# Placing by scatter instead of by matmul, and a new order at the two ends of pass 2

## The chip, the core and the metric

The kernel runs on one core of one Trainium2 chip. The metric is device time in microseconds (us) of one execution. TensorE (PE) multiplies matrices, VectorE (DVE) and ScalarE (ACT) work on rows, GpSimd (POOL) does simple row work and issues indirect DMAs, SyncE (SP) issues plain DMAs. All DMAs share 16 DMA engines.

## The reference, cut to what matters

Four graph layers run one after the other on the same dense float32 adjacency matrix `adj` (2708 x 2708) and features `x` (2708 x 128), each with a residual and a layer norm:

```python
# layer 0: normalised product, 4 nearest neighbours by S, then a second normalised product
z = leaky_relu(lap_mul(A, x) @ W1 + b1, 0.1)
S = exp(-sqrt(max(|zi|^2 + |zj|^2 - 2 zi.zj, 0) + 1e-10) / 2)   # the 4 largest of each row are kept
out0 = lap_mul(S_top4 + A, x) @ W2 + b2          # lap_mul(A, x) = d * (A @ (d * x)), d = 1/sqrt(row sums)
# layer 1: attention over the graph
XW = x @ W; Z = leaky_relu(s_row[:, None] + s_col[None, :], 0.01); den = exp(Z)
num = A @ den
out1 = A @ ((den / num) @ XW)
# layers 2 and 3
out2 = (d * (A @ (d * x))) @ W.T + b;  out3 = relu([x, A @ x] @ W.T + b)
```

In layer 1 `den[i, j]` depends on `s_row[i] + s_col[j]` alone and changes its form where that sum changes sign. If the nodes are sorted by their `s_col` value (`cc` in the kernel), the columns of `den` fall into 43 blocks of 64. For each block most rows keep one form over the whole block; only the few rows whose sign changes inside the block need their own treatment.

## The kernel before, in words

**Passes.** A multiplication with the adjacency matrix is a pass (`by_panels`): `adjT` is walked in C = 6 column chunks (four of 512 columns, one of 384, one of 276). In each chunk T = 22 row tiles of 128 rows (the last of 20) are summed into one PSUM tile `acc`. Rows 0 to 15 come from memory as panels of four tiles (`load_panel`, 1 MB for 512 columns, three buffers, SyncE's queue); rows 16 to 21 stay in SBUF (`res`). So a chunk is 16 matmuls from panels and 6 from `res`, and a 512-column matmul in float32 takes 0.43 us twice.

The stages are: pass 1 with the degrees (L401 to L476), the neighbour search (L524 to L551), pass 2 (L711 to L713), the ranking and pass 3 (L715 to L896), the blocks of the attention (L938 to L968), and three more passes.

**From the search to pass 2.** The search finds for each tile its 4 nearest neighbours (`near`, `where`) by MAX8 and FIND_INDEX8 on VectorE. `weigh(ts)` computes the weights and `y2 = d2inv * x` for a group of tiles and writes these rows to DRAM (`y2_rows`), three times: tiles 0 to 16, 17 to 19, and 20 to 21. The writes are issued from ScalarE's queue (L514, L518). In pass 2, GpSimd gathers four neighbours' rows for every tile from `y2_rows` by indirect DMA (`sum_near`, L571, 88 of them, 16 buffers), and VectorE adds them up (`near_sum`). The first three panels of pass 2 are loaded ahead (`ready`, L520).

**The order by hand.** In pass 2 TensorE, VectorE and ScalarE keep program order (`manual_schedule`). The order is written with `Due`: each pass matmul is a tick, and work is due at a tick. `near_at` says when `sum_near` of a tile is due, and `end_pass2` lays out what follows a finished chunk: `finish` (adds `near_sum` and copies to `hT`), `norm0` (second weight and layer norm), `turn` (transposes), `find_c` (the value `cc` on all partitions, in `c_row`), and for each tile `compare` (which `cc` are at least as large: a mask on VectorE, L664), `times_w` (L651), `rank_rows` (ScalarE adds up the mask's rows, L675) and `rank_columns` (TensorE adds up its columns into `rk`, L680). For the last tile VectorE adds up the rows itself while it makes the mask (L659).

**Ranks, block lists and pass 3.** `rk_f` (L735) is every node's place in the order of `cc`. From it VectorE finds each node's block (`blk`), the weights of pass 3 (`lc`, two columns for each block, in the buffer tagged `wide` that `xwe` had before) and the node's place in the list of its block (`pos`). The lists (`slot_i`, `slot_e`, `slot_f`) are made by matmuls: VectorE writes a 0/1 matrix `at` for each tile (L813) and TensorE multiplies it with the values `val_b` (L814). The order itself is made likewise (`at` L846, matmul L847 with `val_q`), which gives `jidx` (the node at each rank) and `csort` (its `cc`). `xwe` (the rows of XW) is written to `xw_rows`, and 22 indirect DMAs gather its rows in order into `xws` (L857). `rows_from` (L228) puts `csort` and `rr` on all partitions by 44 transposes, for `g_row` and `gb`; `lw` (L865) is made from `g_row`.

Outside pass 2 a scheduler decides the program order of each engine. Pass 3 (L896) multiplies with `lc` and gives `carry`; it runs beside the work of the last paragraph. Then, for each block, GpSimd gathers the list's rows of the matrix (L950), TensorE multiplies them with `lw` (L963), and `mix` divides and multiplies with `xws` (L889).

Of the kernel before, what the change touches and what calls it, by code (L numbers as in the profile page):

```python
# [8 lines left out]
F32 = mybir.dt.float32  # L9
U32 = mybir.dt.uint32  # L10
# [40 lines left out]
def kernel(  # L51
# [105 lines left out]
    def by_panels(weights, done, tick=None, ready=()):  # L157

        ready = list(ready)
        for c in range(C):
            w = cw[c]
            acc = acc_tile()
            for i in range(T):
                if i < S:
                    if i % 4 == 0:
                        part = ready.pop(0) if ready else load_panel(i // 4, c)
                    src = part[:, i % 4, :w]
                else:  # L170
                    src = res[: pw[i], i - S, cols[c]]
                lhsT = weights(i)
                nc.tensor.matmul(  # L173
                    acc[: lhsT.shape[-1], :w], lhsT=lhsT, rhs=src, start=(i == 0), stop=(i == T - 1 and tick is None)
                )
                if i == T - 1:
                    done(c, acc)
                if tick is not None:
                    tick()
# [40 lines left out]
    def rows_from(dst, col, ts, exp_scale=None):  # L220

        ts = list(ts)
        for g in range(0, len(ts), 4):
            grp = ts[g : g + 4]
            ps = mis_tile()
            w = 0
            for t in grp:
                nc.tensor.transpose(  # L228
                    ps[:, w : w + pw[t]], col[: pw[t], t : t + 1].to_broadcast([pw[t], P]), ident[: pw[t], : pw[t]]
                )  # L230
                w += pw[t]
            if exp_scale is None:
                evacuate(g // 4, dst[:, g * P : g * P + w], ps[:, :w])
            else:
                nc.scalar.activation(dst[:, g * P : g * P + w], ps[:, :w], AF.Exp, scale=exp_scale)

# [17 lines left out]
    jidx = att1.tile([P, NQ], U32, tag="jidx", name="jidx")  # L254
# [56 lines left out]
    with tc.tile_pool(name="knn", bufs=1) as knn:  # L311
# [180 lines left out]
        def weigh(ts):  # L492
# [21 lines left out]
            nc.scalar.dma_start(  # L514
                y2_rows[t0 * P : full * P, :].rearrange("(t p) d -> p t d", p=P), y2[:, t0:full, :]
            )
            if full < t1:
                nc.scalar.dma_start(y2_rows[FULL * P :, :], y2[:LAST, FULL, :])  # L518
# [3 lines left out]
        with tc.tile_pool(name="keys", bufs=3) as keys:  # L522
# [28 lines left out]
            weigh(range(T - 2, T))  # L551
# [8 lines left out]
    xwe = wide.tile([P, T, D + 1], F32, tag="wide", name="xwe")  # L560
# [37 lines left out]
    xw_rows = dram.tile([N, D], F32, tag="xw_rows", name="xw_rows")  # L598
# [49 lines left out]
    def times_w(c, t):  # L648
        p, o = pw[t], t * P - starts[c]
        po = mis_tile()  # L650
        nc.tensor.matmul(po[:p, : D + 1], lhsT=xTs[c][:, o : o + p], rhs=wae[:, : D + 1], start=True, stop=True)  # L651
        nc.scalar.copy(xwe[:p, t, :], po[:p, : D + 1])

    def compare(t):
# [3 lines left out]
        if t == T - 1:  # L658
            nc.vector.tensor_scalar(  # L659
                mask[:p, : o + p], c_row[:p, : o + p], s, 0.0, op0=ALU.is_ge, op1=ALU.add,  # L660
                accum_out=rows_m[:p, t : t + 1],
            )
        else:
            nc.vector.tensor_scalar(mask[:p, : o + p], c_row[:p, : o + p], s, None, op0=ALU.is_ge)  # L664
# [5 lines left out]

    def rank_rows(t):
        p, w = pw[t], t * P + pw[t]
        if t < T - 1:
            junk = sum_pool.tile([P, N], BF16, tag="copy", name="junk")
            nc.scalar.activation(junk[:p, :w], masks[t][:p, :w], AF.Copy, accum_out=rows_m[:p, t : t + 1])  # L675
# [12 lines left out]
    near_at = [31 + 4 * t for t in range(4)] + [44 + (24 * (t - 4)) // 5 for t in range(4, 15)]  # L688
    near_at += [100, 106, 113, 120, 128, 135, 142]
# [3 lines left out]
    def end_pass2(c, acc):  # L693
        n = max(T * (c + 1), near_at[chunk_tiles[c][-1]] + 3)

# [5 lines left out]
        at(n + 2, norm0, chunk_tiles[c])  # L701
        at(n + 9, turn, c)
        at(n + 11, find_c, c)
        for k, t in enumerate(chunk_tiles[c]):
            at(n + 13 + 2 * k, compare, t)
            at(n + 14 + 2 * k, times_w, c, t)
            at(n + 16 + 2 * k, rank_rows, t)
            if t:
                at(n + 19 + 2 * k, rank_columns, t)

    with tc.manual_schedule(engines={nc.tensor.engine, nc.vector.engine, nc.scalar.engine}):  # L711
        by_panels(rows_of(y2), end_pass2, due.tick, ready)
        due.flush()  # L713
    late.close()
    lwx = ctx.enter_context(tc.tile_pool(name="lwx", bufs=1))  # L715
    xws = lwx.tile([P, NQ, D], F32, tag="xws", name="xws")
    lw = lwx.tile([P, NB, BJ], F32, tag="lw", name="lw")
    g_row = hT

    with tc.tile_pool(name="rank", bufs=1) as rank, tc.tile_pool(name="rank2", bufs=2) as rank2:  # L720
# [3 lines left out]
        nc.scalar.dma_start(xw_rows[: FULL * P, :].rearrange("(t p) d -> p t d", p=P), xwe[:, :FULL, :D])  # L724
        if LAST:
            nc.scalar.dma_start(xw_rows[FULL * P :, :], xwe[:LAST, FULL, :D])
        nc.vector.tensor_copy(rr, xwe[:, :, D])
        nc.scalar.activation(e_r, rr, AF.Exp)
        nc.scalar.activation(f_r, rr, AF.Exp, scale=0.01)

# [6 lines left out]
        nc.vector.tensor_add(rk_f[:lp, T - 1 :], after[:lp, T - 1 :], rows_m[:lp, T - 1 :])  # L737

# [18 lines left out]
        lc = wide.tile([P, T, NB, 2], F32, tag="wide", name="lc")  # L757
# [32 lines left out]
        totals = rtile([T, NB], "totals")  # L790
# [16 lines left out]
        val_b = big.tile([P, T, 3, NB], F32, tag="y", name="val_b")  # L807
        for n, v in enumerate((node_oob, e_r, f_r)):
            nc.vector.tensor_mul(val_b[:, :, n, :], in_b, v[:, :, None].to_broadcast(grid))
        sl = mis_tile()  # L810
        for t in range(T):
            at = rank2.tile([P, P], F32, tag="at", name="at")
            nc.vector.tensor_scalar(at, iota, pos[:, t : t + 1], None, op0=ALU.is_equal)  # L813
            nc.tensor.matmul(  # L814
                sl[:, : 3 * NB], lhsT=at, rhs=val_b[:, t, :, :].rearrange("p a b -> p (a b)"),
                start=(t == 0), stop=(t == T - 1),
            )
        for h in range(2):
            nc.vector.tensor_scalar(
                slot_i[h], sl[:, :NB], 2.0, 2.0 * OOB + h, op0=ALU.mult, op1=ALU.add  # L820
            )

        nc.vector.tensor_scalar_add(slot_e, sl[:, NB : 2 * NB], ident[:, KC : KC + 1])
        nc.vector.tensor_scalar_add(slot_f, sl[:, 2 * NB : 3 * NB], ident[:, KC + 1 : KC + 2])


        rk_i = rtile([T], "rk_i", I32)
        nc.vector.tensor_copy(rk_i, rk_f)
        hi_i = rtile([T], "hi_i", I32)
        nc.vector.tensor_single_scalar(hi_i, rk_i, 7, op=ALU.arith_shift_right)  # L830
        hi = rtile([T], "hi")
        nc.vector.tensor_copy(hi, hi_i)
        lo = rtile([T], "lo")
        nc.vector.scalar_tensor_tensor(lo, hi, -float(P), rk_f, op0=ALU.mult, op1=ALU.add)
        of_q = rtile([T, NQ], "of_q")
        nc.vector.tensor_tensor(
            of_q, hi[:, :, None].to_broadcast([P, T, NQ]), iota[:, None, :NQ].to_broadcast([P, T, NQ]),
            op=ALU.is_equal,
        )
        val_q = big.tile([P, T, 2, NQ], F32, tag="y", name="val_q")  # L840
        nc.vector.tensor_mul(val_q[:, :, 0, :], of_q, node[:, :, None].to_broadcast([P, T, NQ]))
        nc.vector.tensor_mul(val_q[:, :, 1, :], of_q, cc[:, :, None].to_broadcast([P, T, NQ]))
        js = mis_tile()
        for t in range(T):
            at = rank2.tile([P, P], F32, tag="at", name="at")
            nc.vector.tensor_scalar(at, iota, lo[:, t : t + 1], None, op0=ALU.is_equal)  # L846
            nc.tensor.matmul(  # L847
                js[:, : 2 * NQ], lhsT=at, rhs=val_q[:, t, :, :].rearrange("p a q -> p (a q)"),
                start=(t == 0), stop=(t == T - 1),
            )  # L850
        nc.vector.tensor_copy(jidx, js[:, :NQ])
        nc.vector.tensor_copy(csort, js[:, NQ : 2 * NQ])
        nc.scalar.activation(g_col, csort, AF.Exp, scale=0.99)
        nc.scalar.activation(g_inv, csort, AF.Exp, scale=-0.99)
        for q in range(NQ):
            p = pw[q]
            nc.gpsimd.indirect_dma_start(  # L857
                out=xws[:p, q, :], out_offset=None, in_=xw_rows[:, :],
                in_offset=bass.IndirectOffsetOnAxis(ap=jidx[:p, q : q + 1], axis=0),
                bounds_check=N - 1, oob_is_err=False,  # L860
            )
            nc.scalar.mul(xws[:p, q, :], xws[:p, q, :], g_col[:p, q : q + 1])
        rows_from(g_row, csort, range(T), 0.99)
        for b in range(NB):
# [3 lines left out]
            )  # L868

    gb = hT  # L870
    rows_from(gb, rr, range(T), 0.99)
    carry = big.tile([P, N], F32, tag="y", name="carry")

    def mix(w, q, num, col, haccs, pool):
# [12 lines left out]
        for o in range(0, w, CW):  # L887
            e = min(w, o + CW)
            nc.tensor.matmul(  # L889
                haccs[:, o:e], lhsT=xws[:p, q, :], rhs=err[:p, o:e], start=(q == 0), stop=(q == NQ - 1)  # L890
# [5 lines left out]
    by_panels(lambda i: lc[: pw[i], i, :, :].rearrange("p b s -> p (b s)"), end_carry)  # L896
    psum.close()
# [74 lines left out]

    mixed = big.tile([P, T, D], F32, tag="y", name="mixed")
# [99 lines left out]
```

## Time and profile before

| | us |
|---|---|
| time, median of 3 runs | 1165.31 (1161.83 to 1165.72) |
| the profiled execution | 1204.79 |
| its span, first to last instruction | 1203.1 |
| TensorE busy in the span | 1088.8 (91%) |
| VectorE busy | 657.8 (55%) |
| ScalarE, GpSimd busy | 317.5, 264.9 |
| pass 2 and its tail, in the span | 291 to 487 |
| pass 3 | 490 to 634 |

All other times in the text come from the profiled execution: they are us from the span's start. A timeline line has the start, the length, engine, source line, operation, the names written and read, the shape, how many instructions are merged, and in brackets how long the engine was idle before it and what ended that. "PE" is a matmul, "PEld" its weight load; an engine's name with a q is its sequencer, which issues DMAs. One matmul of the source is two records in float32. "Granted clock" is TensorE's clock as a share of full speed.

### The profile page before, as it was taken

The numbers are of one execution on the slowest core, as the hardware profiler recorded it, in microseconds if no ns is written. First come the engines' busy times: TensorE is split into PE (matmuls) and PEld (weight loads), VectorE is DVE, ScalarE is ACT, GpSimd is POOL, SyncE is SP. The second block draws the span as 40 slices with busy tenths as digits, with TensorE's granted clock in tenths as the row PEclk, the third lists the DMA queues.
The fourth block names the chain that finished last, engine by engine and source line by source line (L and its number), as shares of the span: only waits on it lengthen the run. The fifth ranks groups of instructions, "written<-read, shape, count | busy, mean of one in ns | idle before, by whom it ended". The sixth has DMA issues, their size and how long they took to land. (4 is left out here: it accounts for less than half of the span.)

```text
span 1203.1 us, 11015 instructions
## 1 busy us (share of the span) xinstructions
PE 1088.8 (91%) x3625; PEld 515.5 (43%) x3625; DVE 657.8 (55%) x1428; ACT 317.5 (26%) x591; POOL 264.9 (22%) x261
## 2 busy tenths in 40 slices
PE   1899999999946995796799999999899999999997
PEld 1355444443423473253243333333344554465445
DVE  6875469999215476843005999999712112123122
ACT  0001145554001245104005566666311010002000
POOL 4000000001574670007014555565001000000000
PEclk9899999999977896798799999999899999999999
DMA  9994410002715461541653453455375675664754
GB/s 351 372 296 170 141 35 0 1 1 89 269 48 173 150 205 41 176 147 46 202 159 117 149 168 113 128 163 166 109 245 180 191 263 184 209 205 142 250 169 121
DMA packets 113714, 190.88 MB, mean 159 GB/s; under 512 B 13334, under 2 KB 51520, under 8 KB 113652
## 3 DMA queue, kind: packets, MB, share of 16 engines
q1 hardware_dynamic: 90872, 151.05, 38.1%
q0 software_dynamic: 17280, 36.31, 9.6%
q10 hardware_dynamic: 5500, 2.77, 0.8%
q8 instruction: 30, 0.49, 0.2%
q14 instruction: 32, 0.26, 0.1%
HBM read 214.34 MB, written 4.16 MB: 182 GB/s over the span
## 5 line engine op out<-in xcount | busy, mean ns | idle before, releaser
L173 PE MATMUL acc<-part,y 128*128 128x512 f32 (+2 forms) x384 | 160.0, 560 | 0.5 <-issue 0.5
L950 POOL DMA_INDIRECT rows<-in_adjT,slot_i x86 | 122.2, 1421 | 148.6 <-PE num L963 69.5
L963 PE MATMUL num<-rows,lw 128*64 128x512 f32 (+2 forms) x516 | 115.7, 557 | 2.8 <-DMA rows<-in_adjT,slot_i 2.8
L889 PE MATMUL hacc<-err,xws 128*128 128x512 f32 (+3 forms) x264 | 112.4, 562 | 2.2 <-DVE err L884 2.2
L543 PE MATMUL acc<-zT,z 128*128 128x512 f32 (+4 forms) x264 | 107.1, 551 | 0.0
L571 POOL DMA_INDIRECT got<-y_rows,where x88 | 93.3, 1060 | 58.3 <-DVE near_sum L577 21.7
L173 PEld LDWEIGHTS acc<-part,y 128*128 128x128 f32 x384 | 71.2, 196 | 69.0 <-issue 61.9
L173 PE MATMUL acc<-part,lc 128*86 128x512 f32 (+2 forms) x192 | 84.6, 585 | 16.4 <-DMA part<-in_adjT 13.9
L882 DVE TENSOR_TENSOR err<-inv,num 128x1024 f32<-128x1024 f32 (+1 forms) x88 | 74.3, 855 | 22.4 <-ACT inv L879 21.0
L878 ACT ACTIVATE inv<-num 128x1024 f32<-128x1024 f32 (+1 forms) x88 | 64.4, 735 | 83.1 <-PE num L963 79.2
L544 ACT COPY key<-acc 128x512 f32<-128x512 f32 (+3 forms) x132 | 70.2, 534 | 58.2 <-issue 29.8
L374 PE MATMUL acc<-part,y 128*128 128x512 f32 (+2 forms) x192 | 82.3, 581 | 2.2 <-DVE y L197 2.2
L889 PEld LDWEIGHTS hacc<-err,xws 128*128 128x128 f32 (+1 forms) x264 | 46.6, 189 | 79.7 <-issue 40.4
L173 PE MATMUL acc<-part,xs 128*128 128x512 f32 (+2 forms) x192 | 77.9, 546 | 0.1
L884 DVE SCALAR_TENSOR_TENSOR err<-hT,g_inv,err 128x1024 f32<-128x1024 f32 (+1 forms) x88 | 77.1, 917 | 0.0
L173 PE MATMUL acc<-part,mixed 128*128 128x512 f32 (+2 forms) x192 | 75.5, 545 | 0.1
L883 DVE SCALAR_TENSOR_TENSOR err<-err,inv 128x1024 f32<-128x1024 f32 (+1 forms) x88 | 71.8, 857 | 0.0
L184 ACT COPY hT<-acc 128x512 f32<-128x512 f32 (+2 forms) x18 | 9.6, 535 | 230.1 <-PE acc L173 230.1
L543 PEld LDWEIGHTS acc<-zT,z 128*128 128x128 f32 (+1 forms) x264 | 46.8, 186 | 54.0 <-issue 48.7
L545 DVE MAX8 near<-key 128x8 f32<-128x2708 f32 (+1 forms) x22 | 65.4, 2972 | 5.1 <-ACT key L544 5.1
L879 ACT ACTIVATE inv<-inv 128x1024 f32<-128x1024 f32 (+1 forms) x88 | 67.3, 768 | 2.6
L508 POOL TENSOR_TENSOR y<-xs,d2inv 128x2176 f32<-128x2176 f32 (+1 forms) x2 | 4.7, 2325 | 277.4 <-ACT d2inv L506 277.4
(230 smaller groups left out, 1270.9 us busy)
## 6 DMA issues: line engine op xcount, KB each, us to landing
part<-in_adjT SPq DMA_DIRECT2D x102, 1024.0 KB
part<-in_adjT SPq DMA_DIRECT2D x24, 768.0 KB
part<-in_adjT SPq DMA_DIRECT2D x24, 552.0 KB
res<-in_adjT SPq DMA_DIRECT2D x4, 1280.0 KB
got<-y_rows,where POOLq DMA_INDIRECT x88
rows<-in_adjT,slot_i POOLq DMA_INDIRECT x86
rows<-carry SPq DMA_DIRECT2D x86, 10.6 KB
xw_rows<-xwe ACTq DMA_DIRECT2D x1, 1344.0 KB
```

The source lines that it names most:

```text
L173: nc.tensor.matmul(acc[: lhsT.shape[-1], :w], lhsT=lhsT, rhs=src, start=(i == 0), stop=(i == T - 1 and tick is None))
L374: nc.tensor.matmul(accs[c][:, : cw[c]], lhsT=y[: pw[i], i, :], rhs=src[: pw[i], : cw[c]], start=first, stop=last)
L543: nc.tensor.matmul(pks[c][:p, : cw[c]], lhsT=z2[:, :p], rhs=zT[:, cs], start=False, stop=True)
L544: nc.scalar.copy(key[:p, cs], pks[c][:p, : cw[c]])
L571: nc.gpsimd.indirect_dma_start(out=got[:p, :], out_offset=None, in_=y2_rows[:, :], in_offset=bass.IndirectOffsetOnAxis(ap=where[:p, t, k : ...
L879: nc.scalar.activation(inv[:p], inv[:p], AF.Exp, scale=-1.0)
L882: nc.vector.tensor_mul(err[:p], inv[:p], num[:p, :w])
L883: nc.vector.scalar_tensor_tensor(err[:p], err[:p], 2.0, inv[:p], op0=ALU.subtract, op1=ALU.mult)
L884: nc.vector.scalar_tensor_tensor(err[:p], gb[:p, col : col + w], g_inv[:p, q : q + 1], err[:p], op0=ALU.max, op1=ALU.mult)
L889: nc.tensor.matmul(haccs[:, o:e], lhsT=xws[:p, q, :], rhs=err[:p, o:e], start=(q == 0), stop=(q == NQ - 1))
L950: nc.gpsimd.indirect_dma_start(out=rows[:KC, n, :], out_offset=None, in_=adj_half[:, :], in_offset=bass.IndirectOffsetOnAxis(ap=slot_i[h][ ...
L963: nc.tensor.matmul(num[n * BJ : n * BJ + bw[b], o:e], lhsT=lw[:, b, : bw[b]], rhs=rows[:, n, c0 + o : c0 + e], start=True, stop=True,)
```

## The change

Four parts:

- **Order and lists by scatters.** The matmuls L814 and L847, their matrices, `jidx`, `xw_rows` and the gathers L857 go. `xwe` gets one more column, for `cc`; 22 indirect DMAs on GpSimd write its rows to `by_rank` in DRAM, each row to the place of its rank, and one load brings them back as `xws`, with `csort` in the last column. Another 22 write three values of each node (12 bytes) to `by_slot`, at the place in its block's list, and one load brings the lists back. `rows_from` gives way to `as_row` (one transpose of 22 rows, exponential, write to DRAM) and `on_all` (one load that repeats the row on all partitions). The 22 scalings of `xws` on ScalarE become one product on GpSimd.
- **`lc` in a buffer of its own**, where it shared the one of `xwe`.
- **Last rows ahead.** `weigh` writes tiles 20 and 21 from SyncE's queue, and the first panel load of pass 2 that isn't loaded ahead stands behind that write (`behind`). The other two writes move to GpSimd's queue. In chunk 0 of pass 2 four resident tiles (16 to 19) come before tiles 12 to 15 (`first`).
- **Tail of pass 2.** `near_at` is earlier; what follows chunk 4 is laid between the steps of chunk 5; `times_w` of chunks 3 and 4 is put off; the last tile of chunk 4 (tile 18) also has its rows added up by VectorE (`by_dve`).

```diff
 by_panels:
-            for i in range(T):
+            for n, i in enumerate(first if first and c == 0 else range(T)):
...
+                        elif behind is not None:
+                            with tc.issue_after(behind):
+                                part = load_panel(i // 4, c)
+                            behind = None
 weigh:
+            queue = nc.gpsimd if t1 < T else nc.sync
-            nc.scalar.dma_start(
+            ins = queue.dma_start(
                 y2_rows[t0 * P : full * P, :].rearrange("(t p) d -> p t d", p=P), y2[:, t0:full, :]
...
-    near_at = [31 + 4 * t for t in range(4)] + [44 + (24 * (t - 4)) // 5 for t in range(4, 15)]
-    near_at += [100, 106, 113, 120, 128, 135, 142]
+    near_at = [28, 32, 37, 41] + [42 + (24 * (t - 4)) // 5 for t in range(4, 15)] + [97, 102, 109, 116, 123, 128, 131]
 end_pass2, last chunk (chunk 4 alone keeps norm0, turn, find_c and its first compare):
+            a, b, d = chunk_tiles[C - 2]
+            at(n + 1, rank_rows, a)
+            at(n + 2, compare, b)
+            at(n + 3, rank_rows, b)
+            at(n + 4, norm0, ts)
+            for t in chunk_tiles[C - 3]:
+                at(n + 5, times_w, C - 3, t)
+            at(n + 6, compare, d)
+            at(n + 7, rank_columns, a)
+            at(n + 7, rank_columns, b)
+            at(n + 8, turn, c)
+            at(n + 9, find_c, c)
+            at(n + 10, rank_columns, d)
...
 after pass 2:
+        def as_row(col, name):
+            ps = mis_tile()
+            nc.tensor.transpose(ps[:T, :P], col, ident)
+            lines = rank.tile([T, P], F32, tag=name, name=name)
+            nc.scalar.activation(lines, ps[:T, :P], AF.Exp, scale=0.99)
+            flat = dram.tile([T, P], F32, tag=name + "_d", name=name + "_d")
+            nc.gpsimd.dma_start(flat[:, :], lines)
+            return flat
+        def scatter(out, idx, src):
+            for t in range(T):
+                p = pw[t]
+                ins = nc.gpsimd.indirect_dma_start(
+                    out=out[:, :], out_offset=bass.IndirectOffsetOnAxis(ap=idx[:p, t : t + 1], axis=0),
+                    in_=src[:p, t, :], in_offset=None, bounds_check=out.shape[0] - 1, oob_is_err=False,
+                )
...
+        nc.vector.tensor_copy(rk_u, rk_f)
+        scatter(by_rank, rk_u, xwe)
...
+        nc.vector.scalar_tensor_tensor(pos, pos, float(NB), blk, op0=ALU.mult, op1=ALU.add)
+        nc.vector.tensor_copy(pos_u, pos)
+        scatter(by_slot, pos_u, val)
+        r_row = as_row(rr, "g_r")
+        nc.gpsimd.dma_start(xws[:, : N // P, :], by_rank[: FULL * P, :].rearrange("(q p) d -> p q d", p=P))
...
+        nc.gpsimd.dma_start(slots.rearrange("p b v -> p (b v)"), by_slot.rearrange("(p b) v -> p (b v)", p=P))
...
+        nc.vector.tensor_copy(csort, xws[:, :, D + 1])
+        g_row = on_all("g_row", as_row(csort, "g_c"))
+        nc.gpsimd.tensor_mul(xws[:, :, :D], xws[:, :, :D], g_col[:, :, None].to_broadcast([P, NQ, D]))
         for b in range(NB):
             nc.vector.tensor_scalar(lw[:, b, : bw[b]], g_row[...], slot_e[...], slot_f[...], ...)
+        gb = on_all("gb", r_row)
```

## The prediction

> **What bounds the kernel now.** I read the stage table first, then TensorE's timeline where the table is thin, then VectorE's and GpSimd's timelines to see who is late. In the stage table each line gives a stretch, its length, and the busy time of PE, PEld, DVE, ACT and POOL with instruction counts, then the granted clock, DMA share and GB/s:
>
> ```profile
> 416.00:454.00 38.00, 38.00 (x238) 26.02 (x237) 29.04 (x107) 18.74 (x34) 24.67 (x20) 0.95 0.59 186
> 454.00:490.00 36.00, 13.63 (x148) 10.00 (x147) 26.00 (x80) 16.39 (x27) 0.00 (x0) 0.60 0.15 46
> 490.00:541.00 51.00, 50.65 (x180) 24.74 (x180) 31.13 (x99) 2.15 (x6) 0.00 (x0) 0.95 0.50 165
> 541.00:577.00 36.00, 19.86 (x70) 9.15 (x68) 10.09 (x44) 14.48 (x37) 22.07 (x22) 0.76 0.22 67
> 577.00:634.00 57.00, 55.83 (x151) 23.56 (x152) 1.24 (x2) 0.58 (x1) 5.14 (x5) 0.94 0.56 178
> ```
>
> TensorE sets the time except in two holes. The first, 454 to 490, is the tail of pass 2: TensorE works 13.6 of 36 us, VectorE 26. The second, 541 to 577, is inside pass 3. TensorE's timeline around pass 3:
>
> ```profile
> 482.33 0.72 PE L680 MATMUL rk<-ones_b,mask 20*128 20x1 bf16 x21 [2.53 <-DVE mask L659]
> 487.24 0.63 PE L749 MATMUL mis<-c_part,ones_f 128*128 128x43 f32 x2 [4.20 <-DVE hi L832]
> 490.35 5.09 PE L173 MATMUL acc<-part,lc 128*86 128x512 f32 x6 [2.48 <-DVE lc L776]
> ...
> 515.15 0.61 PE L814 MATMUL mis<-val_b,at 128*128 128x129 f32 x4
> 515.60 1.02 PE L173 MATMUL acc<-part,lc 128*86 128x512 f32 x2
> 516.45 0.61 PE L814 MATMUL mis<-val_b,at 128*128 128x129 f32 x4
> ...
> 577.88 6.55 PE L173 MATMUL acc<-part,lc 128*86 128x512 f32 x8 [13.64 <-DMA part<-in_adjT]
> 584.26 5.47 PE L173 MATMUL acc<-res,lc 128*86 128x512 f32 x12
> ```
>
> See two things: the placing matmuls L814 stand between pass-3 matmuls and lengthen the pass, and after an idle stretch matmuls run at half speed (eight in 6.55 us, then twelve in 5.47). GpSimd's and ScalarE's lines tell when the first gather of neighbours may go, and what an indirect DMA costs:
>
> ```profile
> 302.47 0.34 ACTq L514 DMA_DIRECT2D y_rows<-y  x1
> ...
> 309.89 1.24 POOL L571 DMA_INDIRECT got<-y_rows,where  x1 [9.35 <-DMA y_rows<-y]
> ...
> 541.51 1.01 POOL L857 DMA_INDIRECT xws<-xw_rows,jidx  x1 [89.40 <-DVE carry L146]
> 542.83 1.01 POOL L857 DMA_INDIRECT xws<-xw_rows,jidx  x1 [0.30 <-issue]
> ```
>
> The last write of y2's rows needs 7.4 us, because panel loads stand ahead of it; indirect DMAs of 128 rows follow each other every 1.31 us.
>
> The profiled execution took 1204.8 us, 39.5 more than the median 1165.3. It holds TensorE idles of 15.1 and 10.5 us (333 to 370) and of 13.6 us (before 577.9), 39.2 in sum, all in stretches where GpSimd issues indirect DMAs back to back; the sum is that difference. I take them to belong to that execution, count them in neither kernel, and apply my sum to the median.
>
> **What the Trainium skill says.** "DMA: Bandwidth & Descriptors", section "Anatomy of one DMA — SWDGE (gpsimd) path": a fixed 2.0 us, mostly the write receipt, plus bytes at 436 GB/s. The trace agrees: from the first gather's start (309.89) to its first use (312.70) are 2.8 us. The same page, "Specifications": below 512 B the engine does read-modify-write; the new 12 B rows fall under it and no row of this trace shows such a write. Same page, "Issuing engines are not separate DMA queues": changing the issuing queue alone gains nothing; so only the order ahead of the panels counts. "TensorE: Matmul & The Clock Gate", "Part 1": half clock after an idle window; the 6.55 against 5.47 above agrees.
>
> **The change, part by part.** R is the time the ranks are ready (rk_f, 483.5 plus the new cast, so 483.8 in the old trace).
>
> (1) Tail of pass 2. VectorE carries it: from norm0 of chunk 4 (L619 at 449.73) to rk_f are 33.8 us. It sat idle 1.77 (own, L643), 4.14 (xs, L619) and 2.73 (own) us. The new order puts compares into these gaps: minus 8.6, plus 0.8 for the one wait that stays (find_c of chunk 4). Tile 18's compare now sums its rows itself: L659's 3.02 us for 2708 columns against L664's 1.48 for 2432, so plus 1.2. Sum −6.6. Chunks 3 and 4 also finish 3 and 4 ticks earlier, and VectorE waited 3.91 us for chunk 3 at 434.25: up to −2.5. The moved times_w are as many as before. I take −8; ends −3 and −10.
>
> (2) Last rows ahead of the panels. SP's queue now holds the write (ready 302.4) and behind it panel 3, issued at 294.82 before. The write lands about 2.5 us later, at 305, and the first gather starts 4.8 us earlier. Panel 3 lands about 307 (2.6 us for 1 MB at the 400 GB/s seen here, plus receipt). Chunk 0 takes resident tiles first and needs it at its 17th matmul, 291.1 + 16 × 0.86 = 304.9: 2 us of idle. In exchange chunk 0's wait for near_sum (0.51) and any later wait for gathers go; 88 gathers at 1.31 are 115 us beside a pass of about 130. The other two writes move from ScalarE to GpSimd, where they stand ahead of the gathers but end by 300; ScalarE no longer waits 2.18 us for the product. I take −2; ends −5 and +3.
>
> (3) Placing by scatter. TensorE loses 22 L814 (a pair plus a pass matmul takes 1.30, the matmul alone 0.86: 11 × 0.44 = 4.9), 22 L847 (11 × 0.41 = 4.5) and 44 L228 (44 × 0.113 = 5.0), and gains two transposes: −14.4 + 0.3 = −14.1. VectorE loses L809, L813 and L846 (hidden beside the pass).
>
> (4) The new wait. In the changed kernel's program order TensorE has the transpose of csort after 15 matmuls of pass 3, and csort now comes out of DRAM. Pass 3 starts at R + 6.6 (490.35) and its 15th matmul ended about 506.4: TensorE gets there at R + 22.6. csort's chain: 22 scatters on GpSimd at 1.31 (price of the gather, the nearest row), the last begun at R + 27.5 and landed 2.8 later, R + 30.3; then the load of xws, 2708 rows of 520 B, 1.4 MB. Estimate 7.5 us: 4 at 350 GB/s, 1.5 to issue, 2 receipt. csort is there at R + 38. TensorE idles 15.4 us; all of pass 3 and its panels are queued behind that transpose. Restart at half clock: 6.55 − 3.44 for four tiles, so +3.1. Together +18.5. A scatter cannot be bounded from this trace: at 0.6 us each the wait vanishes; at twice the gather it grows by 28.8.
>
> (5) lc in its own buffer: without it lc would wait for the scatters that read xwe. L776 waited for nothing before, so 0.
>
> (6) Cover behind csort. pos_u is behind the csort copy on VectorE, so GpSimd's product of xws (L508: 3.83 us for 2176 columns, 5.0 for 2816) and 22 scatters of slots run to R + 72, slots and g_row land about R + 83, lw (9.66 us, L865) ends R + 93, then gb and the row gathers. Pass 3 ends at R + 6.6 + 100 + 3 + 1 + 18.5 = R + 129 (132 tiles 100 us, cold start 3, L795's matmuls 1), and the first row gather was issued 7 us before its end (627.64), so R + 122. This has 29 us to spare: 0. If it were gone, each further us would be paid at stage 4's first matmul.
>
> Sum: −8 − 2 − 14.1 + 18.5 = −5.6 us. Forecast **1159.7 us**. A difference under 0.3% (3.5 us) can hardly be told from none.
>
> **Rivals.**
> B, slower: the scatter costs more than the gather. Every 0.1 us adds 2.2 to the wait of (4). For it: writes to DRAM, receipts. Against: 20-row gathers take hardly less than 128-row ones (936 against 997 ns), so issue is mostly fixed cost. It decides from 1.31 + (5.6 + 3.5)/22 = 1.72 us a scatter; at 2.6 us it gives 1159.7 + 28.4 = 1188.
> C, faster: csort arrives in time, as the program order supposes; wait and restart go: 1159.7 − 18.5 = 1141. Against it the 1.31.
> D: the tail doesn't do what it says, VectorE waits elsewhere, (1) gives 0: 1168.
>
> **How the numbers follow.** A (forecast, own range 1148 to 1168): 0.42, of which 0.30 faster, 0.08 same, 0.04 slower. B 0.33, slower. C 0.16, faster. D 0.09: 0.04 same, 0.05 slower. Faster 0.46, same 0.12, slower 0.42. The range from 1140 to 1188 holds A, most of C, and B up to twice the gather.
>
> **What would show it.** Right: one TensorE idle of about 15 us before the csort transpose, released by VectorE's csort, which was released by the xws load; scatters every 1.3 us; tail of pass 2 at 28 us or less; no L814 kin in pass 3. Wrong: scatters over 1.7 us apart, no idle at csort, VectorE gaps in the tail, or stage 4's first matmul waiting for lw, gb or rows.

## The result, and the profile after

| kernel | median us | runs | ratio to the kernel before, 95% interval |
|---|---|---|---|
| before | 1165.06 | 4 | |
| after | 1152.37 | 4 | 0.9895, 0.9874 to 0.9916 |
| after, on a second chip (before there: 1163.15, 41 runs) | 1157.22 | 12 | 0.9933, 0.9909 to 0.9956 |

The change makes the kernel faster by 12.7 us between the medians in the first comparison. In the second it is 7.8 us by the ratio (0.67% of 1163.15) and 5.9 us between the medians. The forecast of −5.6 us lies outside the first interval (−14.7 to −9.8 us) and inside the second (−10.6 to −5.1 us); the two intervals overlap at about 10 us. Below, a difference in us is worked out from the ratio and the median before, unless medians are named.

Chips differ. Experiments 1 to 3 and the first run of experiment 4 are from a chip where the kernel before took 1163.90 us; on the second chip of the table it took 1163.15, on a third 1213.51. The chip of the first comparison is not on record. So a time is compared with the time of a kernel that ran beside it, unless the text says otherwise.

The profiled execution of the kernel after spans 1149.4 us; its 1151.1 us lie close to the median. The stage table of the kernel after, cut at its own stage ends (columns as before: stretch, length, busy time of PE, PEld, DVE, ACT, POOL with counts, then clock, DMA share, GB/s):

```profile
421.00:444.00 23.00, 14.13 (x150) 10.68 (x148) 19.53 (x61) 12.95 (x23) 2.76 (x4) 0.59 0.08 27
444.00:451.00 7.00, 0.70 (x3) 0.58 (x3) 6.12 (x18) 1.04 (x3) 5.49 (x6) 0.50 0.12 39
451.00:467.00 16.00, 16.00 (x35) 5.63 (x35) 14.55 (x42) 2.17 (x5) 12.53 (x12) 0.85 0.57 175
467.00:486.00 19.00, 0.28 (x1) 0.00 (x0) 0.26 (x3) 0.00 (x0) 9.42 (x10) 0.56 0.48 156
486.00:577.00 91.00, 90.73 (x234) 35.79 (x235) 12.37 (x53) 1.76 (x5) 33.80 (x32) 0.98 0.66 212
```

The tail of pass 2 is now 23 us, with VectorE busy in 19.5 of them. One hole remains in pass 3, 467 to 486, where TensorE does next to nothing. TensorE's timeline of the kernel after names it:

```profile
450.92 3.71 PE L181 MATMUL acc<-part,lc 128*86 128x512 f32 x4 [2.47 <-DVE lc L837]
...
459.40 7.89 PE L181 MATMUL acc<-part,lc 128*86 128x512 f32 x18
486.16 0.37 PE L760 MATMUL mis<-ident,csort 128*22 128x128 f32 x1 [18.88 <-DVE pos L872]
486.33 1.92 PE L181 MATMUL acc<-part,lc 128*86 128x512 f32 x2
488.03 6.36 PE L181 MATMUL acc<-res,lc 128*86 128x512 f32 x12
494.33 13.97 PE L181 MATMUL acc<-part,lc 128*86 128x512 f32 x32
```

The releaser is given as pos, a neighbour of csort in VectorE's queue: the copy of csort ended at 486.02 and pos stood behind it. VectorE's timeline shows that it was csort that came late, and GpSimd's shows the chain ahead of it (the second fence):

```profile
485.84 0.18 DVE L892 COPY csort<-xws 128x22 f32<-128x22 f32 x1 [18.74 <-DMA xws<-by_rank]
485.93 0.17 DVE L872 SCALAR_TENSOR_TENSOR pos<-pos,blk 128x22 f32<-128x22 f32 x1
```

```profile
304.84 1.11 POOL L563 DMA_INDIRECT got<-y_rows,where  x1 [3.09 <-DMA y_rows<-y]
...
423.21 0.96 POOL L563 DMA_INDIRECT got<-y_rows,where  x1 [0.30 <-issue]
...
445.43 1.94 POOL L776 DMA_INDIRECT by_rank<-xwe,rk_u  x1 [0.30 <-DVE first L804]
447.68 1.04 POOL L776 DMA_INDIRECT by_rank<-xwe,rk_u  x1 [0.30 <-issue]
449.02 0.98 POOL L776 DMA_INDIRECT by_rank<-xwe,rk_u  x1 [0.30 <-issue]
...
474.91 0.93 POOL L776 DMA_INDIRECT by_rank<-xwe,rk_u  x1 [0.30 <-issue]
477.27 1.49 POOL L877 DMA_DIRECT2D xws<-by_rank  x1 [1.43 <-DMA by_rank<-xwe,rk_u]
```

Most scatters follow each other every 1.29 us, like gathers (1.30); a few take longer, so the mean is 1.40. Ranks at 444.0, last scatter begun at 474.9, landed at 477.2, xws loaded by 485.8.

### The profile page after: what moved, and what is told of

Its sections match the earlier page's. It is cut to its first block, busy times and chain, and to the rows that moved or that the text cites. A ratio compares the mean times of both kernels' runs of the same rounds, so it can differ in the third digit from the quotient of the medians.

```text
span 1149.4 us, 10737 instructions
## 1 busy us (share of the span) xinstructions
PE 1062.2 (92%) x3495; PEld 498.2 (43%) x3495; DVE 643.0 (56%) x1381; ACT 302.9 (26%) x557; POOL 299.7 (26%) x296
## 3 DMA queue, kind: packets, MB, share of 16 engines
q0 software_dynamic: 19136, 42.01, 11.6%
## 4 chain that ended last, share of the span: by engine, by line
PE 47%; DMA 2%; DVE 1%; ACT 0%; issue 0%; DVEq 0%; ACTq 0%
PE acc L181 26%; PE num L996 10%; PE hacc L921 9%; DMA part<-in_adjT 1%; PE mis L231 1%; DMA rows<-carry 1%; PE mis L1053 0%; PE mis L1011 0%; PE mis L1049 0%; PE mis L1023 0%; ACT inv L910 0%; DVE err L915 0%; ACT inv L911 0%; ACT mT L1001 0%; DVE err L916 0%
## 5 line engine op out<-in xcount | busy, mean ns | idle before, releaser
L181 PE MATMUL acc<-part,y 128*128 128x512 f32 (+2 forms) x384 | 155.9, 548 | 2.0 <-DMA part<-in_adjT 1.4
L983 POOL DMA_INDIRECT rows<-in_adjT,slot_i x86 | 119.8, 1392 | 124.2 <-PE num L996 80.1
L563 POOL DMA_INDIRECT got<-y_rows,where x88 | 92.8, 1055 | 29.6 <-issue 9.1
L364 PE MATMUL acc<-part,y 128*128 128x512 f32 (+2 forms) x192 | 81.1, 575 | 3.5 <-DVE y L205 2.2
L181 PE MATMUL acc<-part,lc 128*86 128x512 f32 (+2 forms) x192 | 77.7, 560 | 2.6 <-DVE lc L837 2.5
L916 DVE SCALAR_TENSOR_TENSOR err<-gb,g_inv,err 128x1024 f32<-128x1024 f32 (+1 forms) x88 | 77.1, 917 | 0.0
## 6 DMA issues: line engine op xcount, KB each, us to landing
rows<-carry SPq DMA_DIRECT2D x86, 10.6 KB
```

The source lines that it names most:

```text
L181: nc.tensor.matmul(acc[: lhsT.shape[-1], :w], lhsT=lhsT, rhs=src, start=(n == 0), stop=(n == T - 1 and tick is None))
L364: nc.tensor.matmul(accs[c][:, : cw[c]], lhsT=y[: pw[i], i, :], rhs=src[: pw[i], : cw[c]], start=first, stop=last)
L563: nc.gpsimd.indirect_dma_start(out=got[:p, :], out_offset=None, in_=y2_rows[:, :], in_offset=bass.IndirectOffsetOnAxis(ap=where[:p, t, k : ...
L916: nc.vector.scalar_tensor_tensor(err[:p], gb[:p, col : col + w], g_inv[:p, q : q + 1], err[:p], op0=ALU.max, op1=ALU.mult)
L983: nc.gpsimd.indirect_dma_start(out=rows[:KC, n, :], out_offset=None, in_=adj_half[:, :], in_offset=bass.IndirectOffsetOnAxis(ap=slot_i[h][ ...
```

## The experiments

These marks, read from TensorE's, GpSimd's and VectorE's timelines of each profiled execution, carry most verdicts (us from the span's start; "ranks" is the end of rk_f, "pass 3" its first and the end of its last matmul). The first line is a new profile of the unchanged kernel before. All are from chips where the kernel before took 1163 to 1165 us. One profiled execution need not be typical of its kernel: that of placing only took 1170.1 us against a median of 1164.9, that of the last rows only 1157.1 against 1159.6.

| kernel | pass 2 starts | first gather | last near_sum | ranks | pass 3 | its length | span |
|---|---|---|---|---|---|---|---|
| before, again | 293.0 | 311.3 | 437.5 | 456.3 | 463.1 to 589.7 | 126.6 | 1160.7 |
| tail only | 293.6 | 312.4 | 434.0 | 452.2 | 458.9 to 586.5 | 127.5 | 1157.7 |
| last rows only | 292.3 | 304.9 | 430.8 | 449.6 | 456.3 to 582.5 | 126.2 | 1155.4 |
| placing only, second run | 294.6 | 312.6 | 439.7 | 458.5 | 465.4 to 595.6 | 130.2 | 1168.4 |
| after | 292.2 | 304.8 | 425.9 | 444.0 | 450.9 to 577.4 | 126.5 | 1149.4 |
| before, xws on GpSimd, second run | 292.1 | 310.0 | 437.3 | 456.1 | 462.9 to 583.5 | 120.6 | 1154.5 |
| csort late, second run | 291.6 | 304.2 | 425.5 | 443.7 | 450.6 to 558.7 | 108.1 | 1138.5 |

**1. The kernel before once more**, no edit.

> The kernel before, unchanged, with a new profile. Theory 1 (the three idles of TensorE of 39.2 us in sum were of that one profiled execution): the profiled execution takes 1163 to 1168 us, TensorE runs through 333 to 370 us and through the first panels of pass 3 without idles over 3 us. Theory 2 (they belong to the kernel whenever GpSimd issues indirect DMAs back to back, and the change removed a part of them): the idles are there again, 20 us or more in sum. In either case the length from the last pass-2 matmul of the panels to the ranks (29.5 us before, 22.8 us after) and the length of the stretch with the 44 transposes L228 (14.7 us before) tell how much of the 12.7 us was won in each.

One run took 1162.36 us, with a span of 1160.7. Of the idles of 15.1, 10.5 and 13.6 us none is there in that size; one of 7.2 us is, in pass 2. So theory 2 (20 us or more) falls, and theory 1 (none over 3 us) does not hold whole. TensorE's timeline of this new profile of before, with that idle and the stretch of L228:

```profile
350.55 1.26 PE L631 MATMUL mis<-ident,xs 128*128 128x128 f32 x4 [7.22 <-DVE xs L215]
...
513.85 2.67 PE L228 MATMUL mis<-ident,csort 128*128 128x128 f32 x22
516.45 0.65 PE L228 MATMUL mis<-ident,rr 128*128 128x128 f32 x4
517.47 0.65 PE L228 MATMUL mis<-ident,rr 128*128 128x128 f32 x4 [0.37 <-ACT hT L235]
517.95 1.02 PE L173 MATMUL acc<-part,lc 128*86 128x512 f32 x2
521.36 0.93 PE L228 MATMUL mis<-ident,rr 128*128 128x128 f32 x4 [2.39 <-ACT hT L235]
522.08 1.92 PE L173 MATMUL acc<-part,lc 128*86 128x512 f32 x2
523.79 1.11 PE L228 MATMUL mis<-ident,rr 128*128 128x128 f32 x4
525.40 0.65 PE L228 MATMUL mis<-ident,rr 128*128 128x128 f32 x4 [0.50 <-ACT hT L235]
525.88 1.02 PE L173 MATMUL acc<-part,lc 128*86 128x512 f32 x2
528.10 0.48 PE L228 MATMUL mis<-ident,rr 128*128 128x128 f32 x2 [1.20 <-ACT hT L235]
528.52 6.67 PE L173 MATMUL acc<-part,lc 128*86 128x512 f32 x15
```

The bracket says that TensorE waits for ScalarE's eviction of the transposes into hT, four times, 4.5 us in sum, and the clock falls (two matmuls in 1.92 us). From 513.85 to 528.52 are 14.7 us; six matmul records of pass 3 at 0.43 take 2.6; so the 44 transposes cost 12.1 us, not 5.0. The first profile of the kernel before has the same stretch, 14.7 us from 541.48 to 556.19, so this could have been read before the forecast. ScalarE's timeline of the same profile shows why the eviction is late:

```profile
516.53 0.40 ACT L862 ACTIVATE xws<-xws,g_col 128x128 f32<-128x128 f32 x1 [0.41 <-DMA xws<-xw_rows,jidx]
516.84 0.58 ACT L235 ACTIVATE hT<-mis 128x512 f32<-128x512 f32 x1
518.10 0.40 ACT L862 ACTIVATE xws<-xws,g_col 128x128 f32<-128x128 f32 x1 [0.69 <-DMA xws<-xw_rows,jidx]
519.10 0.40 ACT L862 ACTIVATE xws<-xws,g_col 128x128 f32<-128x128 f32 x1 [0.60 <-DMA xws<-xw_rows,jidx]
520.42 0.40 ACT L862 ACTIVATE xws<-xws,g_col 128x128 f32<-128x128 f32 x1 [0.92 <-DMA xws<-xw_rows,jidx]
520.73 0.58 ACT L235 ACTIVATE hT<-mis 128x512 f32<-128x512 f32 x1
```

Between two evictions stand up to three products of xws, each waiting for its gather at the gathers' pace of 1.3 us.

**2. The tail alone.** Edit of before, due times and order as in the change:

```
+    near_at = [28, 32, 37, 41] + ... + [97, 102, 109, 116, 123, 128, 131]
+    by_dve = (chunk_tiles[C - 2][-1], T - 1)
...
+            at(n + 1, rank_rows, a)
...
```

> The kernel before with nothing but the new order of the tail of pass 2 (due times, which engine sums tiles' rows). The prediction: minus 8 us (1157), the gap closing in VectorE. Rival (after's trace: GpSimd issues 88 gathers without a pause from 304.8 to 424.2 us and VectorE then waits for them): the tail cannot end earlier than the gathers let it, and the gathers start as late as before, so minus 3 to minus 6 us, with VectorE and TensorE waiting for the last gathers for 4 us or more near the end of the pass.

1160.43 us against 1163.90 (22 and 43 runs), ratio 0.9968 (0.9951 to 0.9984): −3.7 us. TensorE's timeline of this kernel near the end of pass 2:

```profile
431.91 0.49 PE L588 MATMUL acc<-ident,near_sum 128*128 128x128 f32 x2 [1.63 <-DVE near_sum L579]
434.07 0.61 PE L588 MATMUL acc<-ident,near_sum 20*128 20x20 f32 x2 [1.67 <-DVE near_sum L579]
```

VectorE's line just ahead of the first of them shows what the sum itself waited for:

```profile
431.50 0.35 DVE L579 SCALAR_TENSOR_TENSOR near_sum<-got,sim,near_sum 128x128 f32<-128x128 f32 x1 [1.86 <-DMA got<-y_rows,where]
```

The rival is borne out. From the last near_sum to the ranks it is 18.2 us (18.8 before), so this part hardly changes; what shrinks is the time from the first gather to the last near_sum, from 126.2 to 121.6 us. The 88 gathers take about the same time everywhere: 120.0 us in before's new profile, 119.8 here, 119.3 in the kernel after. The last near_sum ended 6.3 us after the last gather in before and ends 1.9 us after it here, so little is left for a better order.

**3. The last rows alone.** Edit of before:

```
-            nc.scalar.dma_start(
+            queue = nc.gpsimd if t1 < T else nc.sync
+            ins = queue.dma_start(
...
+                            with tc.issue_after(behind):
+                                part = load_panel(i // 4, c)
```

> The kernel before with nothing but the last rows of y2 written ahead of the panel loads (and chunk 0's tiles in the new order). The prediction: minus 2 us (1163), gathers 4.8 us earlier paid for by 2 us of TensorE idle at panel 3. Rival (gathers set the end of the pass): alone, with the old due times, it brings nothing, 0 to minus 1 us, because the old order asks for each tile's neighbours later than they are there; its worth shows only together with the new tail.

1159.64 us against 1163.90 (22 and 43 runs), ratio 0.9972 (0.9956 to 0.9987): −3.3 us, so the rival falls. By the marks the ranks come 6.1 us earlier after the start of pass 2, but behind pass 3 this profile is 1.9 us longer than before's (572.9 for 571.0). TensorE's timeline of this kernel:

```profile
308.00 3.70 PE L181 MATMUL acc<-part,y 128*128 128x512 f32 x8 [1.72 <-DMA part<-in_adjT]
...
344.14 0.60 PE L641 MATMUL mis<-ident,xs 128*128 128x128 f32 x4
```

The price is where it was foreseen: 1.72 us idle for panel 3 (2 predicted). The gain is at 344.14: the 7.2 us that TensorE waited in the same place in the kernel before are gone. VectorE's timeline of before's new profile shows the cause of that wait: the norm of chunk 0 (L619) stood behind near sums of later tiles, and these waited for gathers.

```profile
346.47 0.35 DVE L579 SCALAR_TENSOR_TENSOR near_sum<-got,sim,near_sum 128x128 f32<-128x128 f32 x1 [1.18 <-DMA got<-y_rows,where]
346.74 1.12 DVE L619 SCALAR_TENSOR_TENSOR xs<-mis,d2inv,xs 128x128 f32<-128x128 f32 x4
```

The first gather started 18.3 us after the start of pass 2 there, and 12.6 us after it here.

**4. csort late.** Edit of after: the transpose, g_row, lw and gb move into the pass,

```
+        def by_csort():
+            g_row = on_all("g_row", as_row(csort, "g_c"))
...
     def end_carry(c, acc):
...
+        if c == 1:
+            gbs.append(by_csort())
```

> The changed kernel, but the transpose of csort, its row on all partitions, lw and gb are issued after the second chunk of pass 3 instead of before it (a program-order position 44 tiles into the pass instead of 15). Theory (TensorE's 18.9 us idle at the csort transpose in after's trace is on the path and nothing else waits for it): minus 19 to minus 21 us against the kernel after, 1132 us, no idle of TensorE in pass 3 over 2 us, and lw ready before stage 4 starts. Rival (the wait is only put off: lw, gb or the first gathers of rows come too late): stage 4's first matmul waits 5 to 15 us, and the kernel lands at 1138 to 1148.

1136.50 us against 1163.90 for before (5 and 43 runs), ratio 0.9762 (0.9733 to 0.9791). The kernel after did not run beside it; against its 1152.37 the medians lie 15.9 us apart, less than the theory's 19 to 21. The rival's wait of 5 to 15 us is not there: stage 4's first matmul follows pass 3 at once. A second time, beside the kernel after:

> The kernel after with the csort transpose, g_row, lw and gb issued after the second chunk of pass 3, now beside the kernel after on the same chip. Theory: 16 to 21 us less than the kernel after, whatever the chip, since the wait of 19 to 21 us before that transpose was there on both chips. Rival: on a chip with stalls in the gathers the wait hides a part of them, and less than 12 us are gained there.

1139.40 us (6 runs); the kernel after 1157.22, before 1163.15; ratio to before 0.9783 (0.9751 to 0.9816). So 17.8 us less than after on the same chip, by the medians; pass 3 is 18.9 us shorter (127.0 and 108.1). TensorE's timeline of the second run:

```profile
486.24 5.47 PE L181 MATMUL acc<-res,lc 128*86 128x512 f32 x12
491.64 0.28 PE L761 MATMUL mis<-ident,csort 128*22 128x128 f32 x1
...
553.68 2.09 PE L181 MATMUL acc<-part,lc 128*86 128x276 f32 x8 [2.56 <-DMA part<-in_adjT]
```

No wait stands at the transpose any more; a wait of 2.6 us for one panel has come up, a little more than the first theory allowed (2). lw ended at 544.6, before pass 3 ends at 558.7: the cover holds. This kernel is the fastest of all.

**5. Placing alone.** Edit of after: the tail and the writing of the last rows put back as in before (the edits of 2 and 3 reversed).

> The kernel after, but with the old tail of pass 2 and the last rows written as in the kernel before: placing by scatters and lc's own buffer alone. The prediction's terms (TensorE -14.1, new wait +18.5): 4.4 us slower, 1168. Rival (TensorE's lost work and stalls in pass 3 are -21, the wait +20.9; pass 3 took 126.6 us in the new profile of the kernel before and 126.5 in that of the kernel after): no change, 1162 to 1165, with an idle of 18 to 20 us before the csort transpose and pass 3 of 126 to 127 us. If this is so, the -12.7 us come from the other two parts alone.

On the third chip 1209.07 us against 1213.51 (12 and 31 runs), ratio 0.9957 (0.9935 to 0.9979): −5.2 us, which neither theory foresaw. TensorE stalled there for 25.1 us in pass 2, in a stretch that this kernel shares with before. The stall is five times the difference, and there is no profile of before from that chip, so the difference cannot be divided into parts. A second time:

> The placing by scatters alone, on another chip than the first time, where stalls of TensorE in the gathers hid its parts. The prediction's terms: +4.4 us against the kernel before. Rival, from the lengths of pass 3 in the two traces without these stalls (126.6 and 126.5 us): 0, within 2 us.

1164.92 us against 1163.15 (14 and 41 runs), ratio 1.0018 (1.0000 to 1.0037): +2.1 us, between the two theories, at whose values (0 and +4.4) the interval ends. TensorE's timeline:

```profile
503.36 0.37 PE L727 MATMUL mis<-ident,csort 128*22 128x128 f32 x1 [21.01 <-DVE pos L839]
503.53 1.91 PE L181 MATMUL acc<-part,lc 128*86 128x512 f32 x2
505.24 7.29 PE L181 MATMUL acc<-res,lc 128*86 128x512 f32 x12
```

The wait is 21.0 us here, and the 14 matmul records behind it take 8.9 us where 14 × 0.43 = 6.0: 23.9 us. Pass 3 is 3.6 us longer than in before's new profile. This execution was the slowest of the 14: GpSimd issued the load of xws 4.0 us after its last scatter (1.4 in the kernel after), so the marks set the wait rather high.

**6. The products of xws on GpSimd.** Edit of before:

```
-            nc.scalar.mul(xws[:p, q, :], xws[:p, q, :], g_col[:p, q : q + 1])
         rows_from(g_row, csort, range(T), 0.99)
+        for p, q0, q1 in ((P, 0, FULL), (LAST, FULL, NQ)):
+            nc.gpsimd.tensor_mul(
...
```

> The kernel before, but the 22 products of xws with g_col, which stand between ScalarE's evictions of the 44 transposes L228 and each wait for a gather, become two products on GpSimd behind the gathers. Theory (the 14.7 us from the first L228 to the last are 5.0 of transposes, 2.6 of pass-3 matmuls and about 7 of stalls and half clock, because ScalarE's queue holds the evictions behind gathers): the stretch shrinks to 8 to 10 us and the kernel by 4 to 7, to 1157 to 1160. Rival (TensorE waits for the eviction itself, 0.58 us of ScalarE for each four transposes, whoever forms the products): 0 to -2.

On the third chip 1207.90 us against 1213.51 (20 and 31 runs), ratio 0.9954 (0.9931 to 0.9977): −5.6 us. A second time:

> The kernel before with the products of xws on GpSimd, again on another chip. The first time the stretch of the 44 transposes L228 shrank from 14.7 us (with 2.6 us of pass-3 matmuls in it) to 6.2 us (with 0.9), so by 6.8 us without these, but TensorE then waited 16.1 us for a panel and nothing was left to see. Theory: without that wait the 6.8 us come out, the kernel takes 4 to 7 us less than before. Rival: something else (panels, stage 4's start) takes them back: 0 to -2.

1157.73 us against 1163.15 (22 and 41 runs), ratio 0.9964 (0.9947 to 0.9981): −4.2 us, as the theory said (−5.4 between the medians). TensorE's timeline of the second run:

```profile
514.24 2.67 PE L228 MATMUL mis<-ident,csort 128*128 128x128 f32 x22
516.84 2.40 PE L228 MATMUL mis<-ident,rr 128*128 128x128 f32 x20
519.07 1.02 PE L173 MATMUL acc<-part,lc 128*86 128x512 f32 x2
520.01 0.48 PE L228 MATMUL mis<-ident,rr 128*128 128x128 f32 x2
520.43 10.10 PE L173 MATMUL acc<-part,lc 128*86 128x512 f32 x23
```

The stretch is 6.2 us, of which 0.9 is pass 3: 5.3 for the 44 transposes, against 12.1. Pass 3 takes 120.6 us, 6.0 less. So nearly 7 us of that stretch in the kernel before were no work of TensorE: its transposes waited for evictions that stood behind ScalarE's products, and its clock fell. The change removes that wait together with the transposes.

**7. Scatters twice.** Edit of after:

```
+                if out is by_rank:
+                    ins = nc.gpsimd.indirect_dma_start(
+                        out=again[:, :], ...
```

> The kernel after with each of the 22 scatters by rank issued a second time, into another DRAM tensor that nobody reads: the cost of a scatter doubled. Theory (the chain of 22 scatters at 1.29 to 1.38 us sets when TensorE goes on, one for one): TensorE's idle before the csort transpose grows from 18.9 us by 22 x 1.29 = 28.4 to about 47, and the kernel takes 1181 us. Rival 1 (issue overlaps the movement of the one before, the chain is set by the landing and the load of xws): idle grows by less than 15 us. Rival 2 (the delay also eats up the cover of lw and gb ahead of stage 4): over 1184.

1236.23 us against 1213.51 (4 and 31 runs), ratio 1.0184 (1.0154 to 1.0214), on the third chip. The edit did more than it was meant to: the scheduler also moved the 22 scatters by slot ahead of the load of xws, and csort's transpose behind 23 more tiles of pass 3 (38 in place of 15), and TensorE waited 28.1 us for a panel ahead of it. So the time tests no theory. The chain it does test: ranks at 487.6 and csort at 585.0 are 97.4 us apart, against 41.8 in the kernel after; 44 more scatters at 1.29 would be 56.8, and 55.6 were measured. So the chain grows with the scatters, nearly one for one.

**8. Three gathers.** Edit of after: `for k in range(TOPK - 1)` in sum_near.

> The kernel after with three of the four neighbours gathered and summed for each node (the fourth is left out): 66 gathers in the place of 88. Theory (in the kernel after, the unbroken stream of gathers from 304.8 to 424.2 us, and VectorE's waits for its last ones, set the end of pass 2): the ranks come 4 to 7 us earlier after the start of pass 2 (151.8 us before, 145 to 148 now), then TensorE's own work is the limit, and the kernel takes 1145 to 1149. Rival (VectorE's chain sets it, gathers are only in time): VectorE's 22 fewer sums of 0.27 us on a chain in which few lie in the tail: 0 to -2 us.

1182.79 us against 1213.51 (4 and 31 runs), ratio 0.9741 (0.9712 to 0.9769), on the third chip, without the kernel after beside it. Pass 2 holds a stall of 18.1 us there, and the last near_sum ended 26 us after the last gather: it says nothing on what bounds the kernel after. Whether fewer gathers would end pass 2 earlier stays open.

**9. The kernel after once more**, no edit.

> The kernel after, unchanged, beside the next three on the same chip, because the chips differ: the kernel before took 1164 us (median) on one and 1213 on another, where TensorE stalls for 16 to 28 us while GpSimd issues indirect DMAs back to back, profiled or not. Theory 1 (the change's gain does not hang on the chip): 12 to 13 us below the kernel before, as measured first. Theory 2 (on a chip with these stalls the change removes some of them, or adds some with its 44 scatters): on such a chip the difference is outside -8 to -18 us. On a chip without them this run only gives the reference.

The second comparison of the table at the top: 7.8 us less, so theory 1 (12 to 13) is missed; theory 2 is for a chip with the long stalls, and this one has none. TensorE's wait at csort is 19.4 us, pass 3 127.0 us. Up to the end of pass 3 this profile agrees with the first within 2 us (287.1 and 285.2 from the start of pass 2). Behind it, in stages whose order the change leaves as it was, it is 8.4 us longer, all of it in the blocks of the attention: the first matmul behind them (L1011) starts 231.4 us after pass 3 in the first profile and 239.8 in this one. csort late shows the same (229.4 in its first profile, 239.3 in its second, on this chip), but placing alone does not (231.7 on this chip; before 229.6). What makes this difference was not found.

## Why the prediction was right or wrong

The direction held, and so did the mechanism of the wait: TensorE stands still before csort's transpose. The wait takes all that TensorE saves in pass 3 (20.9 of 21.0 us), so the gain comes from the tail and the earlier rows. The size was too small by 7.1 us in the first comparison and by 2.2 in the second (0.3 between the medians).

**The step that failed** is the price of the 44 transposes in (3): 5.0 us were put in, and their stretch cost 12.1. In the marks of the kernel after, the change is worth −11.5 us up to the ranks and −0.1 in pass 3, −11.6 where −10 and +4.4 were forecast. Of the 6 us between the sums, about −7 are this price, +2.4 the wait (4), and −1.5 the parts (1) and (2).

- **Before's profiled execution.** Leaving its long idles out of the sum was right: before's new profile has none of 13 to 15 us. That they "belong to that execution" is not shown: on the third chip all four profiled kernels have such idles (last section), and the chip of that profile is not on record. And too much was thrown out with them. The 7.2 us wait for chunk 0's gathers is the kernel's own, and so is the stretch of L228.
- **(1) Tail, −8, and (2) last rows, −2.** Near in the sum, split wrong. Measured alone they are −3.7 and −3.3. Together, on the second chip, after less placing alone is −7.8 − 2.1 = −9.9 (−7.7 between the medians), for −10 forecast. In the marks, from the start of pass 2 to the ranks: 163.3 before, 158.6 with the tail, 157.3 with the rows, 151.8 with both; −4.7, −6.0, −11.5. So the two nearly add up: the tail is worth 4.7 us alone and 5.5 on top of the rows. The failed term of (2) was "chunk 0's wait for near_sum (0.51)": the pass waited 7.2 us. The failed term of (1) was VectorE as the only carrier. From norm0 of chunk 4 to the ranks −6.6 was forecast, and −4.2 came with the tail alone (29.6 us for 33.8), −3.8 in the kernel after (30.0, 414.0 to 444.0; so "28 us or less" was missed). There VectorE waits in this part four times for the last gathers, 3.5 us in sum, where compares were to close its gaps. Ahead of it, for "up to −2.5", norm0 of chunk 4 starts 0.6 us earlier with the tail alone, and 1.6 earlier in the kernel after than with the rows alone.
- **(3) TensorE, −14.1.** This failed most. "44 L228 (44 × 0.113 = 5.0)" took busy time for cost; the stretch cost 12.1. With it the sum is −4.9 − 4.5 − 12.1 + 0.3 = −21.2. The traces agree: pass 3 of after without its wait (18.9 + 2.0 of slow restart) is 105.6 us against 126.6, so −21.0. Experiment 6 shows the cause, by its stretch and by its time. Against its pass 3 of 120.6 us, where the stalls are gone, the 105.6 are 15.0 less, close to the 14.1.
- **(4) The wait, +18.5.** Measured 18.9 + 2.0 = 20.9 in after, 23.9 with placing alone. The term that was short is the chain to csort: 41.8 us after the ranks for 38 predicted. The last scatter began at R + 30.9 for R + 27.5, since the first began 1.4 us after the ranks and some took up to 1.94; the load took 8.6 for 7.5. TensorE's arrival (R + 23.3 for R + 22.6) was close; the restart was 2.0 for 3.1.
- **(3) and (4) together** were given +4.4. In after's marks pass 3 is −0.1, with placing alone +3.6, in time +2.1 (0 to +4.3): two errors of opposite sign nearly cancel here, so the time alone would not have shown them. That the second comparison came so near the forecast is in part this luck.
- **(5) and (6)** held: lc waits as before (2.47 us for VectorE; what a shared buffer would cost was not tried), lw ended at 542.4, 28 us ahead of the first row gather at 570.7 (29 forecast), and stage 4's first matmul comes 1.3 us after pass 3 (its next one waits 3.1 us for carry, in before's new profile 1.6 us for the like).
- **Rivals.** B (scatter dearer) fell: 1.29 us for most, 1.40 in the mean, below 1.72. C (no wait) fell for this kernel, but its world exists: csort late gains the 17.8 us that C gave (18.5). D (tail gives nothing) fell: the tail alone gives −4.7 us in the marks and −3.7 in time.

The prediction left open whether 12-byte rows cost more: below 512 B the DMA engine does a read-modify-write by the Trainium skill ("DMA: Bandwidth & Descriptors", section "Specifications"). In the kernel after, the scatters by slot with 12-byte rows follow each other every 1.29 us and land 2.1 us after issue in the median; those by rank with 520-byte rows follow at the same pace and land after 2.3 us. So no cost of the smaller rows shows here.

## What to carry to other kernels

Price a group of small instructions by the length of its stretch in the timeline, with the brackets in it, not by count times busy time: here that was 12.1 us against 5.0. When a result is fetched through DRAM, place its first consumer in each in-order queue where the fetch has surely landed; one transpose behind 15 matmul tiles of a pass cost 20.9 us, and moving it by 29 matmul tiles gave 17.8 back. Ask what feeds a chain before reordering it: the last near_sum can't come before the 88 gathers are through (about 120 us), so a better order alone brought 4.7 us, and starting the gathers earlier brought 6.0. And measure parts one by one: placing by scatters, the largest edit, brought nothing as it stands (+2.1 us, 0 to +4.3), and pays only with its consumer moved.

## What was not expected of the hardware

On the third chip long idles are neither of the profiler nor of one execution. All four kernels profiled there have one of 18 to 27 us in pass 2 while GpSimd issues gathers, and the median of the kernel before, 31 runs, is 1213.5 us there. The waits of ScalarE in the kernel with placing alone on that chip, from 330 to 366 us:

```profile
ACT hT L692 <- remote: 57.6, 1, 57.6
```

and TensorE's timeline there:

```profile
335.24 0.49 PE L578 MATMUL acc<-ident,near_sum 128*128 128x128 f32 x2 [0.62 <-DVE near_sum L569]
335.57 1.88 PE L181 MATMUL acc<-part,y 128*128 128x512 f32 x4
362.56 2.08 PE L606 MATMUL mis<-w,hT 128*128 128x128 f32 x8 [25.11 <-issue]
```

The last matmul into the tile that ScalarE copies (L578) ended at 335.7. ScalarE's copy began only at 361.92, 26 us later, and the trace names no engine as the releaser ("remote"). TensorE went on with the next chunk until 337.4 and then stood still. Why the copy began so late on this chip and not on the others is open; nothing here was tried against it.
